# Second attention: the diagonal blocks of a chunk mirrored through VectorE and memory, and the turned tiles stored in pieces

## The chip, the cores and the metric

The kernel runs on one core of a Trainium2 chip. The metric is the device time of one execution in microseconds, where lower is better.

## What is computed

The input is x with 8 images of 128 channels and 48 x 48 pixels, that is 2304 tokens for each image. Two layers follow each other:

```python
# layer 0: causal attention over a group-normalised x, with leaky relu after each projection
q, k, v = (lrelu(W @ concat(gn(x), positions) + bias) for the three weights)
x = x + causal_softmax(q.T @ k / sqrt(128)) @ v
# layer 1: plain self attention, then a gated recurrence over the tokens
xh = layernorm(tokens(x))
t  = tokens(x) + softmax(xh @ xh.T) @ xh
wx = batchnorm(layernorm(t) @ W.T)
y[s] = sigmoid(wx[s] + y[s - 1] @ V.T)
out = t + y
```

What matters here is the second attention. Its scores are xh @ xh.T, with the same matrix on both sides, so they are symmetric, and so are their exponentials: the block of exponentials for key block m and query block n is the transpose of the block for key block n and query block m.

## The kernel before, in words

**Tiles.** An image has 2304 tokens in 18 blocks of 128 (P). Three blocks make a chunk of 384 (QC), so there are six chunks j = 0 to 5. Every matmul works on f32 tiles with 128 rows; a score tile is 128 keys by 384 queries, and the output of a chunk gathers in one PSUM tile `o` of 128 channels by 384 queries.

**Order of the work.** For each image the causal attention (class `Causal`) is followed by the second attention (class `Full`), chunk by chunk. The program makes one long list of items. For item n, `begin` issues a score matmul and an exponential on ScalarE (L1217 and L1219 in the second attention, L1018 and L1020 in the causal one). Three items later (LAG = 3) `product` issues the matmul that multiplies this tile into `o` (L1231, causal L1029). Everything else (projections, layer norms, residuals, stores) is put in chains of steps, with estimated costs and due times kept by class `Stream`; a step is emitted when its due time is reached, or earlier when something asks for its result (`st.finish`). The order on each engine is thus fixed when the program is built, and each engine runs its own list in order.

**Use of the symmetry before the change.** In chunk j the items of kind "direct" are those key blocks whose chunk n is at least j: their scores and exponentials are computed. The key blocks of earlier chunks are "turned" items. Their exponentials were computed already, as part of an earlier chunk, and only have to be transposed. The transpose goes in two halves. VectorE turns each 32 x 32 square of a direct tile (L1188) and puts the result in a tile `t`, which gathers three of them, 576 KB. The squares themselves change place by a trip through memory: `store` writes `t` to a DRAM tile `e` with one transfer (L1168), and `load` reads `e` back to a tile `g` with four transfers, one for each group of 32 partitions (L1159). The product of a turned item (L1227) reads `g` in place of a fresh exponential. There are 15 such pairs of chunks for each image. Two `t` tiles and three `g` tiles exist, so a transpose waits for the store of two tiles before, and a load waits for the products of three tiles before.

**The diagonal chunk.** The three key blocks of chunk j itself are direct items of full width: three score matmuls, three exponentials and three products of 384 columns each. The blocks behind the diagonal of this 3 x 3 square are computed twice, once on each side. For j > 0 these three items come last in their chunk.

**Transfers.** All transfers of the two attentions are issued by SyncE (SP), in order. Each transfer carries one of eight landing counters in turn, and in the built program it waits until the transfer that carried the same counter before it has landed. Between the attention and the recurrence each chunk also goes through `residual`, `rooted`, `spread` (three transfers `rs<-roots_t`, L1291, and four `t_d<-tt`, L1294), `fetch` (`t2x<-t_d`, L1298, and `scale<-rs`, L1300) and `product` (the matmul `wx<-t2x`, L1306, the ScalarE copy `t2c<-t2x`, L1327, and the VectorE product `scale<-wx`, L1307). The causal attention has a path of its own, `token_major`, that is of the same form as the new one: 192 KB to memory in one transfer (`o_d_c<-ot_c`, L966), then back in four of 48 KB (`to_c<-o_d_c`, L972). In `project`, VectorE adds the position term from PSUM to a work tile `z` (L884) and applies the leaky relu from `z` to its destination (L889).

Of the kernel before, what the change touches and what calls it, by code (L numbers as in the profile page):

```python
# [14 lines left out]
F32 = mybir.dt.float32  # L15
AF = mybir.ActivationFunctionType
ALU = mybir.AluOpType
# [587 lines left out]
def fast_path(ctx: ExitStack, tc: tile.TileContext, x, pe, w_ffn, out, x_tok, w_qkv, w_pos, v_t, gamma_beta, flag):  # L605
# [61 lines left out]
    with ExitStack() as actx:  # L667
# [24 lines left out]
        def chunk_tile(tag, name, holder=None, steps=0, bufs=2):  # L692

            if holder is not None:
                before = holders.setdefault(tag, deque([({}, 0)] * bufs))
                old, n = before.popleft()
                before.append((holder, steps))
                if "chain" in old:
                    st.advance(old["chain"], n)
            return (work if bufs == 2 else work1).tile([P, QC], F32, tag=tag, name=name)  # L700
# [154 lines left out]
        def project(b, n):  # L855

            cols = ts(n, QC)
            c = {}

            def normed():  # L860
                if n > 1:
                    st.finish(projected[b, n - 2])
                if (b, n) in pos_loads:
                    st.finish(pos_loads[b, n])
                c["pb"] = pos.pop((b, n))
                if n == 0:
                    keys[b] = big.tile([P, N], F32, tag="k", name=f"k_{b}")
                    vals[b] = big.tile([P, N], F32, tag="vT", name=f"vT_{b}")
                    largest[b] = small2.tile([P, 2, NQ], F32, tag="largest", name=f"largest_{b}")
                mg, rs = norm_of[b]  # L870
                c["xn"] = chunk_tile("xn", f"xn_{b}_{n}", c, 4)
                nc.vector.tensor_scalar(c["xn"], xbuf[b][:, cols], mg, rs, ALU.subtract, ALU.mult)  # L872

            def part(j):
                def f():
                    xn = c["xn"]
                    ps = psum_s(f"pj_{b}_{n}_{j}")
                    if j < 2:
                        nc.tensor.matmul(ps[:, :QC], wT[:, j, :], xn, start=True, stop=True)  # L879
                    else:  # L880
                        for m in range(0, QC, P):
                            nc.tensor.matmul(ps[:, ds(m, P)], xn[:, ds(m, P)], wT[:, j, :], start=True, stop=True)  # L882
                    z = chunk_tile("z", f"z_{b}_{n}_{j}")
                    nc.vector.tensor_add(z, ps[:, :QC], c["pb"][:, j, :])  # L884
                    if j == 0:
                        queries[b, n] = qp.tile([P, QC], F32, tag="q", name=f"q_{b}_{n}")
                    dst = (queries[b, n], keys[b][:, cols], vals[b][:, cols])[j]

                    nc.vector.scalar_tensor_tensor(dst, z, 0.01, z, ALU.mult, ALU.max)  # L889
                    c[j] = dst  # L890
                    if j == 2:
                        for i in range(2):
                            nc.vector.tensor_reduce(
                                largest[b][:, i, n : n + 1], c[i], AX.X, ALU.max, apply_absolute_value=True
                            )
                        load_positions(*divmod(b * NQ + n + 2, NQ))
                        if n + 1 < EARLY:
                            project(b, n + 1)
                        if n == NQ - 1 and b + 1 < B:
                            st.add([(partial(load_x, b + 1), 0.0, [])], 5.0)  # L900

                return f

            steps = [(normed, 0.0, [("DVE", 0.75)])]

            steps += [(part(j), QC * US, [("DVE", 0.0 if j < 2 else 4.5)]) for j in range(3)]
            c["chain"] = projected[b, n] = st.add(steps)
# [76 lines left out]
        def listed(chunks):  # L984
            return [(j, w, i == 0, i == len(ws) - 1) for j, ws in enumerate(chunks) for i, w in enumerate(ws)]
# [143 lines left out]
        class Full:  # L1129
# [12 lines left out]
            @staticmethod  # L1142
            def items():
                chunks = []
                for j in range(NQ):
                    behind = list(range(j + 1, NQ))
                    ahead = [("direct", QB * n + g) for n in ([0] + behind if j == 0 else behind + [j]) for g in range(QB)]
                    turn = [("turned", i, g) for i in range(j) for g in range(QB)]
                    both = [((k + 0.5) / len(ahead), w) for k, w in enumerate(ahead)]
                    both += [((k + 0.5) / len(turn), w) for k, w in enumerate(turn)]  # L1150
                    chunks.append([w for _, w in sorted(both, key=lambda e: e[0])])
                return listed(chunks)

            def load(self):
                i, j = self.pairs[len(self.loaded)]
                d, _ = self.stored[i, j]
                g = gpool.tile([P, R, QB, QB, SQ], F32, tag="g", name=f"g_{self.b}_{i}_{j}")
                for r in range(R):
                    nc.sync.dma_start(  # L1159
                        g[ts(r, SQ)].rearrange("c a j m r -> c a (j m r)"),  # L1160
                        d.rearrange("(a c) b f -> b c a f", a=R)[r],
                    )
                self.loaded[i, j] = g

            def store(self):
                j, n, t, at = self.to_store.popleft()
                d = dpool.tile([P, R, QB * QB * SQ], F32, tag=f"e_{j}_{n}", name=f"e_{self.b}_{j}_{n}")
                nc.sync.dma_start(d, t.rearrange("p b j m r -> p b (j m r)"))  # L1168
                self.stored[j, n] = d, max(at, st.now)

            def prefetch(self):
                while self.to_store and self.to_store[0][3] <= st.now:
                    self.store()
                n = len(self.loaded)
                if n < len(self.pairs) and n < self.used + 3 and self.pairs[n] in self.stored:
                    if self.stored[self.pairs[n]][1] + 6.0 <= st.now:
                        self.load()

            def turned(self, j, m, p, ready):

# [15 lines left out]
            def begin(self, j, what, first):  # L1196
                b = self.b
                if j == 0:
                    st.finish(normed_chunks[b, what[1] // QB])
                if first and b + 1 < B:  # L1200
                    if j == 1:
                        norm_chain[b + 1] = st.add(group_norm(b + 1))
                    if j == NQ - 2:
                        st.finish(norm_chain[b + 1])
                        project(b + 1, 0)
                self.prefetch()
                if what[0] == "turned":
                    i, g = what[1:]
                    while (i, j) not in self.loaded:
                        while self.pairs[len(self.loaded)] not in self.stored:  # L1210
                            self.store()
                        self.load()
                    return self.loaded[i, j][:, :, g, :, :].rearrange("p a m r -> p m a r"), 0.0
                m = what[1]
                xh = x_hat[b][1]
                s = psum_s(f"s1_{b}_{j}_{m}")
                nc.tensor.matmul(s[:, :QC], xh[:, ts(m, P)], xh[:, ts(j, QC)], start=True, stop=True)  # L1217
                p = pp.tile([P, QC], F32, tag="p", name=f"p1_{b}_{j}_{m}")
                nc.scalar.activation(p, s[:, :QC], AF.Exp, bias=shift)  # L1219
                return p, st.then(st.spend(QC * US), [("ACT", 0.5)])  # L1220

            def product(self, j, what, o, p, ready, first, last):
                xhT = x_hat[self.b][0]
                if what[0] == "turned":
                    i, g = what[1:]
                    out_ap = o[:, :QC].rearrange("p (m a r) -> p m a r", m=QB, a=R)
                    nc.tensor.matmul(out_ap, xhT[:, QB * i + g, :], p, start=first, stop=last)  # L1227
                    if g == QB - 1:
                        self.used += 1
                else:  # L1230
                    nc.tensor.matmul(o[:, :QC], xhT[:, what[1], :], p, start=first, stop=last)  # L1231
                    if what[1] // QB > j:
                        self.turned(j, what[1], p, ready)
                st.spend(QC * US, ready)

            def after(self, j, o):
                b = self.b
# [379 lines left out]
```

## Time and profile before

| | before |
|---|---|
| median of 3 runs | 1761.54 us (1758.81 to 1763.01) |
| the profiled execution's own time | 1763.07 us |
| span in its profile | 1761.4 us |
| TensorE matmul busy | 1733.7 us, 98% of the span |
| VectorE busy | 1159.5 us, 66% |
| ScalarE busy | 718.9 us, 41% |
| GpSimd busy | 321.0 us, 18% |
| mean granted TensorE clock | 0.991 |
| the 16 DMA engines: share of the queue that SyncE feeds | 50.3% |
| exponentials of the second attention (L1219) | 504, 580 ns each |
| exponentials of the causal attention (L1020), 384, 256 and 128 wide | 490, 384 and 277 ns each |
| transposes `t<-p` (L1188) | 360, 550 ns each |

The profile comes from one execution. "PE" is TensorE's matmul, "PEld" its weight load, "DVE" VectorE, "ACT" ScalarE, "POOL" GpSimd and "SP" SyncE; a "q" behind the name stands for the engine's queue of instructions that wait or issue transfers. A group of instructions is named by its source line, its engine and "what it writes <- what it reads". An f32 matmul of this kernel stands in the profile as two records, so a count of 1008 means 504 matmuls. Ends of matmuls are modelled and overlap the next, so the time that a matmul really takes is read from one start to the next.

### The profile page before, as it was taken

The numbers are of one execution on the slowest core, as the hardware profiler recorded it, in microseconds if no ns is written. First come the engines' busy times: TensorE is split into PE (matmuls) and PEld (weight loads), VectorE is DVE, ScalarE is ACT, GpSimd is POOL, SyncE is SP. The second block draws the span as 40 slices with busy tenths as digits, with TensorE's granted clock in tenths as the row PEclk, the third lists the DMA queues.
The fourth block names the chain that finished last, engine by engine and source line by source line (L and its number), as shares of the span: only waits on it lengthen the run. The fifth ranks groups of instructions, "written<-read, shape, count | busy, mean of one in ns | idle before, by whom it ended". The sixth has DMA issues, their size and how long they took to land.

```text
span 1761.4 us, 21442 instructions
## 1 busy us (share of the span) xinstructions
PE 1733.7 (98%) x6134; PEld 1082.0 (61%) x6135; DVE 1159.5 (66%) x3163; ACT 718.9 (41%) x1332; POOL 321.0 (18%) x397
## 2 busy tenths in 40 slices
PE   8999999999999999999999999999999999999986
PEld 5666666656666566666666566665666666665565
DVE  4875569655886459755696557864587556974357
ACT  2344334443344424443244433444344432444345
POOL 1131002300132001410024001320014100240006
PEclk7999999999999999999999999999999999999998
DMA  3415673157533684156731575335941568216768
GB/s 128 144 32 185 174 202 117 63 178 208 161 93 110 182 223 138 41 178 178 205 117 61 181 203 158 99 111 175 229 140 41 172 178 211 62 56 181 204 214 217
DMA packets 206050, 261.94 MB, mean 149 GB/s; under 512 B 90113, under 2 KB 175010, under 8 KB 205412
## 3 DMA queue, kind: packets, MB, share of 16 engines
q1 hardware_dynamic: 204972, 257.47, 50.3%
q0 software_dynamic: 720, 2.62, 1.0%
q8 instruction: 51, 0.84, 0.2%
q14 instruction: 75, 0.61, 0.1%
q10 hardware_dynamic: 232, 0.40, 0.1%
HBM read 150.24 MB, written 110.17 MB: 148 GB/s over the span
## 4 chain that ended last, share of the span: by engine, by line
PE 96%; DMA 1%; DVE 1%; SPq 1%; issue 0%; ACT 0%; POOL 0%; DVEq 0%; ACTq 0%; POOLq 0%
PE s L1217 18%; PE o L1231 18%; PE s L1018 17%; PE o L1029 17%; PE o L1227 13%; PE pj L879 4%; PE pj L882 2%; PE z L1530 2%; PE wx L1306 2%; PE tb L939 1%; PE of_t L939 1%; PE pb L837 0%; DMA x<-in_x_dram 0%; PE dn L1077 0%; DMA t2x<-t_d 0%; DMA out_dram<-r 0%
## 5 line engine op out<-in xcount | busy, mean ns | idle before, releaser
L1219 ACT ACTIVATE p<-s,shift 128x384 f32<-128x384 f32 x504 | 292.5, 580 | 519.0 <-PE s L1217 497.8
L1217 PE MATMUL s<-xh 128*128 128x384 f32 x1008 | 409.3, 488 | 0.0
L1020 ACT ACTIVATE p<-s 128x384 f32<-128x384 f32 (+2 forms) x504 | 231.0, 460 | 427.3 <-PE s L1018 349.3
L1231 PE MATMUL o<-p,xhT 128*128 128x384 f32 x1008 | 402.4, 486 | 1.1 <-ACT p L1219 1.1
L1018 PE MATMUL s<-q,k 128*128 128x384 f32 (+2 forms) x1008 | 382.9, 462 | 0.2 <-DVE k L889 0.2
L1029 PE MATMUL o<-p,vT 128*128 128x384 f32 (+2 forms) x1008 | 378.3, 457 | 0.0
L1227 PE MATMUL o<-g,xhT 128*128 128x384 f32 x720 | 281.4, 486 | 1.1 <-DMA g<-e 1.1
L1188 DVE STREAM_TRANSPOSE t<-p 128x384 f32<-128x384 f32 x360 | 186.1, 550 | 136.2 <-ACT p L1219 97.6
L1231 PEld LDWEIGHTS o<-p,xhT 128*128 128x128 f32 x1008 | 190.2, 190 | 129.2 <-ACT p L1219 1.7
L1217 PEld LDWEIGHTS s<-xh 128*128 128x128 f32 x1008 | 187.4, 190 | 119.5
L1029 PEld LDWEIGHTS o<-p,vT 128*128 128x128 f32 x1008 | 188.5, 191 | 116.1 <-POOL p L1023 3.0
L1018 PEld LDWEIGHTS s<-q,k 128*128 128x128 f32 x1008 | 182.3, 191 | 96.7 <-issue 1.3
L1044 DVE TENSOR_TENSOR acc<-acc,p 128x384 f32<-128x384 f32 (+2 forms) x408 | 213.4, 523 | 26.5 <-POOL p L1023 2.9
L1227 PEld LDWEIGHTS o<-g,xhT 128*128 128x128 f32 x720 | 134.1, 190 | 87.7 <-issue 1.8
L1023 POOL TENSOR_TENSOR p<-p,triu 128x128 f32<-128x128 f32 x144 | 77.8, 544 | 528.9 <-ACT p L1020 527.6
L884 DVE TENSOR_TENSOR z<-pj,pb 128x384 f32<-128x384 f32 x144 | 79.4, 551 | 137.5 <-PE pj L879 120.3
L1280 POOL TENSOR_TENSOR roots<-ve_f,mhalf 128x3 f32<-128x3 f32 x48 | 42.0, 876 | 500.7 <-DVE ve_f L923 500.7
L1114 POOL TENSOR_SCALAR xhT<-xhT 128x384 f32<-128x384 f32 x48 | 60.8, 1267 | 187.5 <-PE tb L939 187.5
L879 PE MATMUL pj<-xn,wT 128*128 128x384 f32 x192 | 80.6, 505 | 1.4 <-DVE xn L872 1.4
L1307 DVE TENSOR_TENSOR scale<-wx,scale 128x384 f32<-128x384 f32 x46 | 25.6, 556 | 69.2 <-PE wx L1306 59.9
L1258 DVE TENSOR_REDUCE dn<-of_t 128x3 f32<-128x384 f32 x48 | 26.6, 554 | 67.5 <-PE of_t L939 67.5
L1115 POOL TENSOR_SCALAR t1t<-t1t 128x384 f32<-128x384 f32 x48 | 61.3, 1277 | 0.0
(237 smaller groups left out, 1469.9 us busy)
## 6 DMA issues: line engine op xcount, KB each, us to landing
e<-t SPq DMA_DIRECT2D x120, 576.0 KB
g<-e SPq DMA_DIRECT2D x480, 144.0 KB
pb<-posb_d SPq DMA_DIRECT2D x46, 576.0 KB
t1t<-in_x_tok_dram SPq DMA_DIRECT2D x48, 192.0 KB
t_d<-tt SPq DMA_DIRECT2D x184, 48.0 KB
t2x<-t_d SPq DMA_DIRECT2D x46, 192.0 KB
scale<-rs SPq DMA_DIRECT2D x46, 192.0 KB
x<-in_x_dram SPq DMA_DIRECT2D x14, 576.0 KB
```

What stands on the lines that cost most here:

```text
L879: nc.tensor.matmul(ps[:, :QC], wT[:, j, :], xn, start=True, stop=True)
L884: nc.vector.tensor_add(z, ps[:, :QC], c["pb"][:, j, :])
L1018: nc.tensor.matmul(s[:, off:QC], keys[b][:, ts(m, P)], queries[b, j][:, off:], start=True, stop=True)
L1020: nc.scalar.activation(p[:, off:], s[:, off:QC], AF.Exp, scale=SCALE)
L1023: nc.gpsimd.tensor_mul(p[:, off : off + P], p[:, off : off + P], triu)
L1029: nc.tensor.matmul(o[:, off:QC], vals[b][:, ts(m, P)], p[:, off:], start=first, stop=last)
L1044: nc.vector.tensor_add(a[:, off:], a[:, off:], p[:, off:])
L1188: nc.vector.transpose(t[:, :, :, g, :].rearrange("p b j r -> p j b r"), p.rearrange("p (j b r) -> p j b r", j=QB, b=R))
L1217: nc.tensor.matmul(s[:, :QC], xh[:, ts(m, P)], xh[:, ts(j, QC)], start=True, stop=True)
L1219: nc.scalar.activation(p, s[:, :QC], AF.Exp, bias=shift)
L1227: nc.tensor.matmul(out_ap, xhT[:, QB * i + g, :], p, start=first, stop=last)
L1231: nc.tensor.matmul(o[:, :QC], xhT[:, what[1], :], p, start=first, stop=last)
```

## The change

(Lines of new steps are those of the changed kernel.) The diagonal chunk no longer computes both sides. Of its three key blocks, block g now covers only the query blocks g and after: the score matmul, the exponential and the direct product are 384, 256 and 128 columns wide (`offset`). What is missing are the blocks (0,1), (0,2) and (1,2), mirrored. For these, `mirror` lets VectorE turn the 32 x 32 squares of the first two tiles (L1187, one transpose of 128 x 256 and one of 128 x 128) into a tile `tm`; one transfer of 192 KB writes it to memory (`m<-tm`, L1200), and four of 48 KB read it back with the squares moved (`gm<-m`, L1203). These five transfers are issued by ScalarE. Two items of a new kind, "mirrored", stand at the end of each chunk; their products (L1271) are 128 and 256 columns wide and read `gm`.

The chunk's own three blocks now come first among its direct items. The turned tiles are now written in four transfers, one for each group of 32 partitions, each in rows of 1152 bytes (L1170), and read back in one, in rows of 4608 bytes (L1162). In `project` the tile `z` is gone: the sum is written to its destination, and the leaky relu works there in place.

```diff
-                    z = chunk_tile("z", f"z_{b}_{n}_{j}")
-                    nc.vector.tensor_add(z, ps[:, :QC], c["pb"][:, j, :])
...
-                    nc.vector.scalar_tensor_tensor(dst, z, 0.01, z, ALU.mult, ALU.max)
+                    nc.vector.tensor_add(dst, ps[:, :QC], c["pb"][:, j, :])
+                    nc.vector.scalar_tensor_tensor(dst, dst, 0.01, dst, ALU.mult, ALU.max)
...
-                    behind = list(range(j + 1, NQ))
-                    ahead = [("direct", QB * n + g) for n in ([0] + behind if j == 0 else behind + [j]) for g in range(QB)]
+                    ahead = [("direct", QB * n + g) for n in range(j, NQ) for g in range(QB)]
...
-                    chunks.append([w for _, w in sorted(both, key=lambda e: e[0])])
+                    order_of = [w for _, w in sorted(both, key=lambda e: e[0])]
+                    first = order_of.index(ahead[0])
+                    order_of.insert(0, order_of.pop(first))
+                    chunks.append(order_of + [("mirrored", g) for g in range(1, QB)])
...
+            @staticmethod
+            def offset(j, m):
+                return max(0, m - QB * j) * P if m < QB * (j + 1) else 0
 
             def load(self):
...
-                for r in range(R):
-                    nc.sync.dma_start(
-                        g[ts(r, SQ)].rearrange("c a j m r -> c a (j m r)"),
-                        d.rearrange("(a c) b f -> b c a f", a=R)[r],
-                    )
+                nc.sync.dma_start(g.rearrange("p a j m r -> p (a j m r)"), d.rearrange("p a f -> p (a f)"))
...
             def store(self):
...
-                nc.sync.dma_start(d, t.rearrange("p b j m r -> p b (j m r)"))
+                turned = d.rearrange("(b c) a f -> a c b f", b=R)
+                for r in range(R):
+                    nc.sync.dma_start(turned[r], t[ts(r, SQ)].rearrange("c b j m r -> c b (j m r)"))
...
+            def mirror(self, j, g, p, ready):
+
+                b, left = self.b, QB - 1 - g
+                if g == 0:
+                    self.tm = chunk_tile("tm", f"tm_{b}_{j}", bufs=1).rearrange("p (b q r) -> p b q r", b=R, q=QB)
+                first = g * (QB - 1)
+                nc.vector.transpose(
+                    self.tm[:, :, first : first + left, :].rearrange("p b q r -> p q b r"),
+                    p[:, (g + 1) * P :].rearrange("p (q b r) -> p q b r", q=left, b=R),
+                )
+                at = st.then(ready, [("DVE", 0.17 + left * 0.13)])
+                if g < QB - 2:
+                    return
...
+                def out_of():
+                    nc.scalar.dma_start(d, tm.rearrange("p b q r -> p b (q r)"))
+
+                def back_in(r):
+                    nc.scalar.dma_start(
+                        gm[ts(r, SQ)].rearrange("c a q r -> c a (q r)"), d.rearrange("(a c) b f -> b c a f", a=R)[r]
+                    )
+
+                steps = [(partial(back_in, r), 0.0, [("ACT", 0.4)]) for r in range(R - 1)]
+                steps = [(out_of, 0.0, [("ACT", 0.4), ("", 3.5)]), *steps, (partial(back_in, R - 1), 0.0, [("ACT", 0.4), ("", 3.5)])]
+                self.moved = st.add(steps, at + 0.6 - st.now)
...
+                if what[0] == "mirrored":
+                    st.finish(self.moved)
+                    return self.gm.rearrange("p a q r -> p q a r"), 0.0
                 m = what[1]
+                off = self.offset(j, m)
...
-                nc.tensor.matmul(s[:, :QC], xh[:, ts(m, P)], xh[:, ts(j, QC)], start=True, stop=True)
+                nc.tensor.matmul(s[:, off:QC], xh[:, ts(m, P)], xh[:, j * QC + off : (j + 1) * QC], start=True, stop=True)
...
-                nc.scalar.activation(p, s[:, :QC], AF.Exp, bias=shift)
+                nc.scalar.activation(p[:, off:], s[:, off:QC], AF.Exp, bias=shift)
...
+                elif what[0] == "mirrored":
+                    g = what[1]
+                    cols = g * P
+                    out_ap = o[:, :cols].rearrange("p (m a r) -> p m a r", m=g, a=R)
+                    nc.tensor.matmul(out_ap, xhT[:, QB * j + g, :], p[:, g - 1 : 2 * g - 1], start=first, stop=last)
                 else:
-                    nc.tensor.matmul(o[:, :QC], xhT[:, what[1], :], p, start=first, stop=last)
-                    if what[1] // QB > j:
+                    off = self.offset(j, what[1])
+                    cols = QC - off
+                    nc.tensor.matmul(o[:, off:QC], xhT[:, what[1], :], p[:, off:], start=first, stop=last)
+                    g = what[1] - QB * j
+                    if g >= QB:
                         self.turned(j, what[1], p, ready)
+                    elif g < QB - 1:
+                        self.mirror(j, g, p, ready)
```

More of the change, by code (lines that the diff above doesn't have):

```diff
@@ L1177, in prefetch @@
                         self.load()
+            def mirror(self, j, g, p, ready):
[10 more added lines that the diff above has]
+                    return
+                gm = chunk_tile("gm", f"gm_{b}_{j}", bufs=1).rearrange("p (a q r) -> p a q r", a=R, q=QB)
+                self.gm = gm
+                d = dpool.tile([P, R, QB * SQ], F32, tag=f"m_{j % 2}", name=f"m_{b}_{j}")
+                tm = self.tm
+                def out_of():
[7 more added lines that the diff above has]
+                self.moved = st.add(steps, at + 0.6 - st.now)
             def turned(self, j, m, p, ready):
@@ L1213, in begin @@
                     return self.loaded[i, j][:, :, g, :, :].rearrange("p a m r -> p m a r"), 0.0
+                if what[0] == "mirrored":
+                    st.finish(self.moved)
+                    return self.gm.rearrange("p a q r -> p q a r"), 0.0
                 m = what[1]
+                off = self.offset(j, m)
                 xh = x_hat[b][1]
                 s = psum_s(f"s1_{b}_{j}_{m}")
-                nc.tensor.matmul(s[:, :QC], xh[:, ts(m, P)], xh[:, ts(j, QC)], start=True, stop=True)
+                nc.tensor.matmul(s[:, off:QC], xh[:, ts(m, P)], xh[:, j * QC + off : (j + 1) * QC], start=True, stop=True)
                 p = pp.tile([P, QC], F32, tag="p", name=f"p1_{b}_{j}_{m}")
-                nc.scalar.activation(p, s[:, :QC], AF.Exp, bias=shift)
-                return p, st.then(st.spend(QC * US), [("ACT", 0.5)])
+                nc.scalar.activation(p[:, off:], s[:, off:QC], AF.Exp, bias=shift)
+                return p, st.then(st.spend((QC - off) * US), [("ACT", 0.17 + (QC - off) * 0.00085)])
             def product(self, j, what, o, p, ready, first, last):
@@ L1229, in product @@
                         self.used += 1
[L1230 to L1232 removed]
+                    cols = QC
+                elif what[0] == "mirrored":
[3 more added lines that the diff above has]
+                    nc.tensor.matmul(out_ap, xhT[:, QB * j + g, :], p[:, g - 1 : 2 * g - 1], start=first, stop=last)
+                else:
+                    off = self.offset(j, what[1])
[3 more added lines that the diff above has]
+                    if g >= QB:
                         self.turned(j, what[1], p, ready)
[L1234 removed]
+                    elif g < QB - 1:
+                        self.mirror(j, g, p, ready)
+                st.spend(cols * US, ready)
             def after(self, j, o):
```

## The prediction, made before the changed kernel ran

> **What bounds the kernel now.** I read the first part of the page, then the slices, the chain, the groups.
>
> ```profile
> PE 1733.7 (98%) x6134; PEld 1082.0 (61%) x6135; DVE 1159.5 (66%) x3163; ACT 718.9 (41%) x1332; POOL 321.0 (18%) x397
> ...
> PEclk7999999999999999999999999999999999999998
> ...
> PE 96%; DMA 1%; DVE 1%; SPq 1%; issue 0%; ACT 0%; POOL 0%; DVEq 0%; ACTq 0%; POOLq 0%
> ...
> L1231 PE MATMUL o<-p,xhT 128*128 128x384 f32 x1008 | 402.4, 486 | 1.1 <-ACT p L1219 1.1
> ...
> L1227 PE MATMUL o<-g,xhT 128*128 128x384 f32 x720 | 281.4, 486 | 1.1 <-DMA g<-e 1.1
> ```
>
> TensorE is the bound: 96% of the chain is its own, at nearly full clock, and its groups hardly ever sat idle (1.1 us each in the whole span). So a column of matmul saved is time saved, unless a new wait appears. What a column costs stands in the order of time (TensorE, causal attention):
>
> ```profile
> 57.16 0.59 PE L1029 MATMUL o<-p,vT 128*128 128x256 f32 x2
> 57.59 0.81 PE L1018 MATMUL s<-q,k 128*128 128x384 f32 x2
> 58.24 0.38 PE L1029 MATMUL o<-p,vT 128*128 128x128 f32 x2
> 58.46 0.81 PE L1018 MATMUL s<-q,k 128*128 128x384 f32 x2
> ```
>
> From start to start: 0.43 us for 256 columns, 0.65 for 384 (0.645 over longer runs), 0.22 for 128. It is proportional; narrow matmuls carry no extra.
>
> Next the queue that feeds the turned tiles: SyncE from chunk 3 to chunk 4 of the fourth image, then memory by chunk (stretches of chunks 3 and 4; last columns clock, DMA share, GB/s).
>
> ```profile
> 821.21 3.01 SPq L1337 DMA_DIRECT2D t2l_d<-t2c  x1
> 824.31 1.57 SPq L1291 DMA_DIRECT2D rs<-roots_t  x3
> 825.93 1.86 SPq L1294 DMA_DIRECT2D t_d<-tt  x4
> 827.89 0.38 SPq L1168 DMA_DIRECT2D e<-t  x1
> 828.36 4.22 SPq L1159 DMA_DIRECT2D g<-e  x8
> ```
>
> ```profile
> 808.20:827.30 19.10, 19.10 (x63) 11.35 (x62) 8.03 (x24) 7.97 (x13) 0.85 (x1) 1.00 0.63 159
> 827.30:848.30 21.00, 21.00 (x77) 13.05 (x76) 13.48 (x34) 6.12 (x9) 0.85 (x1) 1.00 0.96 230
> ```
>
> SyncE issues without a gap for over 11 us, and memory is 96% busy in chunk 4. Setting each load's landing (the last update of its counter in the trace) against its first product, the median margin over 8 images is 1.3 us for pair (1,4), 1.9 for (2,4), 1.1 for (2,5), and 8 or more in chunks 0 to 3. TensorE is covered, but thinly, in chunks 4 and 5. The `wx<-t2x` matmul has margins of 5 to 10 us in chunks 0 to 3 of an image.
>
> **What the Trainium skill says.** "TensorE: Matmul & The Clock Gate", Back-to-back issue gap: in a stream of weight loads and matmuls a narrow one costs more than its share. The trace disagrees (0.22 against 0.65 us), so the trace is used. "DMA: Bandwidth & Descriptors", Anatomy of one DMA: a wait for a semaphore happens on the issuing sequencer before dispatch. The trace agrees: the waits list has SyncE waiting 32.3 us in 18 waits for `o_d_c<-ot_c`. On ScalarE such a wait will hold the exponentials behind it. The same page, Issuing engines are not separate DMA queues: all issuers share the same 16 engines, so a second issuer saves only issue time. No run here shows it.
>
> **Part by part.**
>
> *Matmul columns.* A diagonal chunk had 3 scores and 3 products of 384, that is 2304. It now has 768 of scores, 768 of direct and 384 of mirrored products, 1920. 384 fewer, 48 chunks: 48 x 0.645 = 31.0 us off TensorE. Six matmuls become eight, which by the proportion above costs nothing.
>
> *ScalarE.* Two of three exponentials shrink. By L1020's widths (490, 384, 277 ns) that is 0.32 us a chunk, 15 us in all, hidden. Added are 240 issues, 0.36 us for the 192 KB form (ScalarE's own `wT` load) and 0.43 for the 48 KB form (`to_c`, median): 2.1 us a chunk, 100 in all. At 41% busy there is room. Behind them wait exponentials, whose products are due three items later: 1.9 us in turned stretches, 3.9 in direct ones, less 0.8 for hand-over and exponential. Singly the issues fit; four in a row (1.7 us) come only where the next exponential belongs to the next chunk. I take nothing; if a landing is awaited for over 2 us there, the excess is TensorE's.
>
> *VectorE.* `t<-p` at 384 takes 550 ns, a 32-wide one (L1285) 183; in proportion 0.42 and 0.28. 48 x 0.70 = 34 us, 66% becomes 68%. Hidden; the DVE was idle over a third of these stretches. If late, `m<-tm` waits and ScalarE with it. Dropping `z`: same two operations, nothing, and a few nanoseconds either way at most.
>
> *The mirror's latency.* The `o_d_c`/`to_c` pair has the same sizes: landing 1.6 us after the end of the issue (90% under 2.6), then 1.57 after the last of four (90% under 2.9). In the built order chunks 0 and 1 have a margin. In chunk 3 the last exponential is given off about 3.0 us before the mirrored product; four issues take 1.7, landing 1.6: 0.3, say 0.4 us late. Chunks 2 and 4 come out even, chunk 5 a little early, except at the end of the last image, where nothing follows: 1.5 us late. Low end zero; with the 90% value 1.3 us more in each of four chunks, 5 us an image.
>
> *Stores and loads.* A store goes from one issue (0.38) to four (1.8), a load from four to one. Sum equal: 0. In chunks 4 and 5 there are about 9 loads and 3 stores, so SyncE gains some 8 us of issue there. Packets of 1152 bytes hold an engine 78 ns, of 4608 bytes 206 (mean of the trace's packet records), so a load costs 512 x 78 / 16 = 2.5 us before and 128 x 206 / 16 = 1.65 after; chunk 4's 96% falls to about 75%. Stores get 0.85 dearer in chunks 0 to 2, with DMA shares of 0.36 to 0.60. `t` is freed 2 us later: VectorE already waits 37.3 us for `e<-t`; six `p` buffers cover 3 items more. Nothing on the path.
>
> *What is late next.* The built order shows two new ties. A transfer waits for the one eight before it, and ScalarE's now count among them, so SyncE, which ran 6 to 14 us ahead of TensorE, must wait for transfers that ScalarE issues at TensorE's pace. And the chunk's own blocks come first, so stores stand directly ahead of loads. Pair (1,4): its product moves from 94.6 us after the image's first score to 89.8 (2.6 from four shorter chunks, 2.2 from order). Ahead of its load: the third `rs` waits for the mirror's first read of chunk 3, done at 83.5; four `t_d` 1.9, four stores 1.8, issue 0.35, landing 3.4 to 4.1 (`pb<-posb_d`, same 576 KB form: quiet 3.4, median 4.1). Sum 91.0 to 91.7, late by 0.8 to 1.5 after chunk 3's 0.4; I take 1.1. Pair (2,5): four stores behind late transposes, `t2x`, `scale`, then 3.8: 0 to 1, take 0.4. `t2x` of chunk 0, used in chunk 2: behind two fourfold stores, the second bound to `m<-tm`: 0 to 1, take 0.4.
>
> *Sum.* Give-back for an image 0.4 + 1.1 + 0.4 + 0.4 = 2.3 us, times 8 is 18.4, and 1.5 at the end: 19.9. 1763.1 (span 1761.4 and 1.7 around it) - 31.0 + 19.9 = 1752.0. This run stood 1.5 above the median of the runs shown, so 1750.5, rounded to 1750.
>
> **The rivals.** *Nearly all is kept.* For it: lighter memory in chunk 4 may bring landings to the quiet end, and TensorE's own delays let SyncE catch up. At 0.3 us an image plus 1.5: 1763.1 - 31.0 + 3.9 - 1.5 = 1734.5.
>
> *Slower: the lock-step of two queues.* ScalarE waits for SyncE's landings and SyncE for ScalarE's, through the shared counters; each late landing moves the loads of chunks 3 to 5. For it: SyncE's gapless run, margins of 1.1 to 1.9, five links a chunk. Against it: in the trace the transfer eight back had landed over 5 us before ScalarE's place in 95% of places. It decides from 31.0 / 8 = 3.9 us an image. With each of the waits above 1 us longer (landings near their 90% values) and chunks 2 and 4 late as well, 5.5 us an image: 1763.1 - 31.0 + 44 - 1.5 = 1774.6.
>
> *No change*: 3.5 to 4.3 us an image, 1758 to 1765. That the change doesn't do what it says can't be: the built order has 384 columns fewer in each chunk.
>
> **Numbers.** 0.2% is about what a measurement of this kernel can tell from no change (3.5 us). Partly kept, 1740 to 1758: 0.36. Nearly all kept: 0.20. Same: 0.10. Slower: 0.34, because several places with thin margins must all hold. So faster 0.56, and the time is 1750. The range goes from 1733 to 1774, leaving out a sliver of the best case and nearly half of the slower one; the likeliest case's own range is 1740 to 1758.
>
> **What would show it.** Right: TensorE's busy time without idle falls by 31; L1271 waits for `gm<-m` under 1 us a chunk; L1263 waits for `g<-e` about 12 us in all, in chunk 4; DMA share of chunk 4 near 0.75. Wrong: exponentials (L1255) waited for by products for more than a few us; the `wx` matmul waiting for `t2x` over 1 us an image; waits for `g<-e` in chunks 1 to 3.

## The result and the profile after

The changed kernel takes 1810.94 us in the median of 4 runs (1806.44 to 1816.5). The kernel before takes 1760.17 us on the same chip (1758.35 to 1763.01). The ratio is 1.0289 with a 95% interval of 1.0264 to 1.0315, so the change costs 51 us, where a gain of 11 was forecast (1761.54 to 1750). The profiled execution took 1816.5 us, with a span of 1814.8 us.

The first part, the chain and the groups that matter, from the page of the changed kernel (last columns of a group: busy time and mean of one, then idle time before it and what ended it):

```profile
PE 1725.2 (95%) x6327; PEld 1098.6 (61%) x6327; DVE 1185.4 (65%) x3259; ACT 699.3 (39%) x1332; POOL 319.2 (18%) x397
...
PE 76%; DMA 16%; SPq 3%; DVE 2%; issue 1%; ACT 0%; ACTq 0%; POOL 0%; DVEq 0%; POOLq 0%
...
L1275 PE MATMUL o<-p,xhT 128*128 128x384 f32 (+2 forms) x1008 | 371.6, 457 | 3.4 <-ACT p L1255 3.4
L1263 PE MATMUL o<-g,xhT 128*128 128x384 f32 x720 | 286.8, 497 | 36.9 <-DMA g<-e 36.9
L1220 DVE STREAM_TRANSPOSE t<-p 128x384 f32<-128x384 f32 x360 | 184.1, 550 | 165.4 <-DMA e<-t 141.0
```

TensorE's own share of the chain fell from 96% to 76%, and 16% are now transfers. The product of the turned tiles (L1263) stood still 36.9 us where it had waited 1.1 us before. The other two lines are there for what they don't show: late exponentials cost the direct product 3.4 us, once, and waits of VectorE for stores, 141 us here, turn out below to cost nothing of themselves.

Where the turned tiles come late is seen in SyncE's queue, in the same place of the fourth image as in the prediction (the changed kernel in order of time; start, length):

```profile
836.15 0.34 SPq L1162 DMA_DIRECT2D g<-e  x1
842.39 0.40 SPq L1383 DMA_DIRECT2D out_dram<-t2c  x1
842.84 2.14 SPq L1384 DMA_DIRECT2D t2l_d<-t2c  x1
845.08 1.57 SPq L1338 DMA_DIRECT2D rs<-roots_t  x3
846.69 1.86 SPq L1341 DMA_DIRECT2D t_d<-tt  x4
848.65 1.82 SPq L1170 DMA_DIRECT2D e<-t  x4
850.57 0.38 SPq L1162 DMA_DIRECT2D g<-e  x1
```

From 836.49 to 842.39 SyncE issues nothing. What it waits for is in the waits list of its queue (total, times, longest):

```profile
SPq L1170 <- DMA gm<-m: 39.7, 36, 6.3
SPq L1383 <- DMA m<-tm: 39.6, 7, 5.8
SPq L1170 <- DMA m<-tm: 38.8, 7, 6.6
SPq L1338 <- DMA gm<-m: 25.4, 14, 3.7
```

The store of `out` (L1383) needs nothing that the mirror made. It carries the landing counter that `m<-tm` carried before it, and so it waits until that write of ScalarE's has landed, in seven images of eight for about 5.7 us. (Here `m<-tm`, issued at 836.17, landed at 842.33, and the store went out at 842.39.) Behind it stand 8 us of issues, and then the load of pair (1,4). On TensorE that is the stall at 855.69 (start, length, idle before):

```profile
852.34 0.38 PE L1253 MATMUL s<-xh 128*128 128x128 f32 x2
852.56 0.60 PE L1275 MATMUL o<-p,xhT 128*128 128x256 f32 x2
855.69 1.69 PE L1263 MATMUL o<-g,xhT 128*128 128x384 f32 x4 [2.54 <-DMA g<-e]
857.17 1.49 PE L882 MATMUL pj<-wT,xn 128*128 128x128 f32 x6
858.45 1.49 PE L1253 MATMUL s<-xh 128*128 128x384 f32 x2
859.73 0.63 PE L1275 MATMUL o<-p,xhT 128*128 128x128 f32 x2
860.16 0.93 PE L1353 MATMUL wx<-t2x,w1T 128*128 128x384 f32 x2
```

Two things are to be seen. The wait is 2.54 us. And after it the score matmul of 384 columns at 858.45 takes 1.28 us to the next start, not 0.645: TensorE runs at half speed for a while (the last section has the clock).

### The profile page after: what moved, and what is told of

Read it like the earlier page. It is cut to its first block, busy times and chain, and to the rows that moved or that the text cites. A ratio compares the mean times of both kernels' runs of the same rounds, so it can differ in the third digit from the quotient of the medians.

```text
span 1814.8 us, 22185 instructions
## 1 busy us (share of the span) xinstructions
PE 1725.2 (95%) x6327; PEld 1098.6 (61%) x6327; DVE 1185.4 (65%) x3259; ACT 699.3 (39%) x1332; POOL 319.2 (18%) x397
## 4 chain that ended last, share of the span: by engine, by line
PE 76%; DMA 16%; SPq 3%; DVE 2%; issue 1%; ACT 0%; ACTq 0%; POOL 0%; DVEq 0%; POOLq 0%
PE s L1016 16%; PE o L1027 16%; PE s L1253 13%; PE o L1275 12%; DMA g<-e 7%; PE o L1263 7%; DMA gm<-m 3%; PE pj L879 3%; DMA m<-tm 2%; DMA t2x<-t_d 2%; PE pj L882 2%; PE z L1577 2%; PE o L1271 2%; PE wx L1353 1%; SPq L1170 1%
## 5 line engine op out<-in xcount | busy, mean ns | idle before, releaser
L1255 ACT ACTIVATE p<-s,shift 128x384 f32<-128x384 f32 (+2 forms) x504 | 274.3, 550 | 588.3 <-PE s L1253 469.4
L1253 PE MATMUL s<-xh 128*128 128x384 f32 (+2 forms) x1008 | 381.7, 461 | 0.0
L1275 PE MATMUL o<-p,xhT 128*128 128x384 f32 (+2 forms) x1008 | 371.6, 457 | 3.4 <-ACT p L1255 3.4
L1263 PE MATMUL o<-g,xhT 128*128 128x384 f32 x720 | 286.8, 497 | 36.9 <-DMA g<-e 36.9
L1263 PEld LDWEIGHTS o<-g,xhT 128*128 128x128 f32 x720 | 133.9, 193 | 120.4 <-DMA g<-e 47.1
L886 DVE TENSOR_TENSOR q<-pj,pb 128x384 f32<-128x384 f32 x48 | 26.7, 556 | 94.1 <-PE pj L879 89.1
L927 POOL TENSOR_TENSOR rs_c<-ve_c,mhalf 128x3 f32<-128x3 f32 x48 | 48.4, 1008 | 75.3 <-DVE ve_c L921 75.3
L1271 PE MATMUL o<-gm,xhT 128*128 128x128 f32 x192 | 46.0, 336 | 13.5 <-DMA gm<-m 11.0
```

What stands on the lines that cost most here:

```text
L1253: nc.tensor.matmul(s[:, off:QC], xh[:, ts(m, P)], xh[:, j * QC + off : (j + 1) * QC], start=True, stop=True)
L1255: nc.scalar.activation(p[:, off:], s[:, off:QC], AF.Exp, bias=shift)
L1271: nc.tensor.matmul(out_ap, xhT[:, QB * j + g, :], p[:, g - 1 : 2 * g - 1], start=first, stop=last)
L1275: nc.tensor.matmul(o[:, off:QC], xhT[:, what[1], :], p[:, off:], start=first, stop=last)
```

## The experiments

Four theories were held against each other. A: the two queues are tied through the shared counters, so SyncE falls to the pace of ScalarE's transfers. B: the new form of store and load does it. C: the order with the chunk's own blocks first does it. D: the trip of the mirrored squares is simply too long. M (bytes), S (ScalarE held up) and O (the planner's new order for SyncE) joined later. All times are medians of 4 runs, `swap_alone` of 20 and `mirror_on_tensor` of 12; the ratio is to the kernel before, which stood at 1759.9 to 1760.9 us beside them.

| kernel | us | ratio, 95% interval |
|---|---|---|
| swap_alone | 1757.3 | 0.9979 to 0.9993 |
| order_alone | 1771.6 | 1.0043 to 1.0076 |
| mirror_alone | 1856.6 | 1.0533 to 1.0568 |
| no_trip | 1729.6 | 0.9805 to 0.9838 |
| mirror_on_gpsimd | 1791.2 | 1.0154 to 1.0188 |
| mirror_on_sync | 1832.0 | 1.0385 to 1.0420 |
| trip_unused | 1810.2 | 1.0249 to 1.0309 |
| trip_in_two | 1780.3 | 1.0093 to 1.0127 |
| plan_only | 1743.6 | 0.9871 to 0.9916 |
| trip_small | 1796.6 | 1.0161 to 1.0229 |
| count_only | 1805.1 | 1.0231 to 1.0266 |
| mirror_on_tensor | 1764.4 | 1.0016 to 1.0040 |
| trip_kept_order | 1823.3 | 1.0341 to 1.0382 |
| gpsimd_kept_order | 1795.6 | 1.0147 to 1.0207 |
| tensor_kept_order | 1744.5 | 0.9884 to 0.9917 |

### The parts one by one

`swap_alone`, on the kernel before (the same in `load`, reversed):

```diff
-                nc.sync.dma_start(d, t.rearrange("p b j m r -> p b (j m r)"))
+                turned = d.rearrange("(b c) a f -> a c b f", b=R)
+                for r in range(R):
+                    nc.sync.dma_start(turned[r], t[ts(r, SQ)].rearrange("c b j m r -> c b (j m r)"))
```

> The kernel before, with only the form of the turned tiles' transfers changed: store in four transfers, load in one. No mirror, full-width diagonal, old order. Theory A (the new transfers of ScalarE tie SyncE to TensorE's pace, so loads of turned tiles come late): the swap needs the tie to hurt, so 1757 to 1765 us, waits for g<-e under 5 us. Theory B (the swap itself: four stores stand ahead of the loads, and t is freed later): 1780 to 1800 us, with L1220's counterpart waiting over 100 us for e<-t. Theory C (own blocks first): as A, 1757 to 1765.

1757.3 us: theory B is out for the swap by itself. The waits that looked costly are there all the same (page of `swap_alone`):

```profile
L1186 DVE STREAM_TRANSPOSE t<-p 128x384 f32<-128x384 f32 x360 | 183.4, 548 | 166.6 <-DMA e<-t 114.9
L1225 PE MATMUL o<-g,xhT 128*128 128x384 f32 x720 | 281.3, 487 | 0.9 <-DMA g<-e 0.9
```

VectorE waits 114.9 us for stores (37.3 before) and TensorE notices nothing. VectorE is not the bottleneck.

`order_alone`, on the kernel before:

```diff
-                    behind = list(range(j + 1, NQ))
-                    ahead = [("direct", QB * n + g) for n in ([0] + behind if j == 0 else behind + [j]) for g in range(QB)]
+                    ahead = [("direct", QB * n + g) for n in range(j, NQ) for g in range(QB)]
```

> The kernel before, with only the order changed: the chunk's own three key blocks come first among its direct items, full width, no mirror, transfers as before. Theory A: 1758 to 1766 us. Theory B: 1757 to 1765. Theory C (own blocks first put the finished t tiles, and so their stores, directly ahead of the loads for chunks 4 and 5): 1775 to 1800 us, with waits for g<-e of over 15 us.

1771.6 us, between A's and C's figures: with loads in four pieces the order alone costs 12 us. Together with the new loads it costs next to nothing, as `no_trip` shows.

`mirror_alone` is the changed kernel with the old `store` and `load`, the two edits of `swap_alone` turned round.

> The changed kernel with the old form of the turned tiles' transfers: store in one transfer, load in four. Mirror, narrow matmuls and own-first order stay, ScalarE issues the mirror's transfers. Theory A: the tie is whole, 1795 to 1815 us. Theory B: the loss goes, 1735 to 1755 us. Theory C: 1790 to 1810.

1856.6 us, worse than A expected. B is refuted in sign as well: under the tie the new form of the transfers saves 46 us (1856.6 - 1810.9). Its lines in the waits list of SyncE's queue:

```profile
SPq L1163 <- DMA g<-e: 50.1, 66, 2.7
...
SPq L1163 <- DMA gm<-m: 36.3, 11, 5.4
```

A load in four pieces carries four counters, so it waits for others four times. That the saving comes from there alone was not separated.

`no_trip`, on the changed kernel (the DRAM tile, the five transfers and their steps go too; cut here):

```diff
-                gm = chunk_tile("gm", f"gm_{b}_{j}", bufs=1).rearrange("p (a q r) -> p a q r", a=R, q=QB)
-                self.gm = gm
...
-                self.moved = st.add(steps, at + 0.6 - st.now)
+                self.gm = self.tm
```

> The changed kernel without the mirror's five transfers: the mirrored products read VectorE's tile of turned squares directly, so their squares are in the wrong places, which leaves that part of the computation out. Everything else stays (narrow matmuls, own-first order, store in four, load in one). Theory A: with the tie gone nearly the whole saving shows, 1730 to 1742 us. Theory B: the loss of the swap stays, 1785 to 1805 us. Theory C: likewise 1780 to 1800.

1729.6 us, as A had it. The page of `no_trip`:

```profile
PE 1703.0 (99%) x6327; PEld 1099.2 (64%) x6327; DVE 1186.1 (69%) x3259; ACT 698.5 (40%) x1332; POOL 309.6 (18%) x397
...
PE 97%; DVE 1%; DMA 1%; ACT 0%; issue 0%; POOL 0%; SPq 0%; ACTq 0%; POOLq 0%; DVEq 0%
...
L1247 PE MATMUL o<-g,xhT 128*128 128x384 f32 x720 | 278.3, 487 | 0.8 <-DMA g<-e 0.8
```

TensorE is busy 30.7 us less than before (1733.7), and the time fell by 30.3 (from 1759.9 beside it). The whole saving is there, with the narrow matmuls, the own-first order, VectorE's transposes and the new stores and loads all in. What takes it away is the trip, with the steps that plan it. In the profiled executions `no_trip` and the changed kernel are 86 us apart. TensorE's stalls are 68 us longer in the changed kernel, by the starts of its matmuls, and slow matmuls after stalls cost it 12.5 us more (last section). That accounts for 81 of the 86.

### What of the trip it is

`mirror_on_sync` and `mirror_on_gpsimd` change who issues the five transfers (`nc.sync` or `nc.gpsimd` for `nc.scalar`).

> The changed kernel with the mirror's five transfers issued by SyncE. Theory A: SyncE now waits for tm and for m in its own order, so it is tied to TensorE's pace in the same way, 1790 to 1840 us. Theory D: 1795 to 1820. Theory M: 1800 to 1815. Theory S: ScalarE is free of it, 1730 to 1745 us.

> The changed kernel with the mirror's five transfers issued by GpSimd, whose transfers carry eight landing counters of their own in the built program. Theory A (tie of SyncE to ScalarE through the shared counters): the tie is gone while bytes and trip stay, 1730 to 1745 us. Theory D (the trip's own latency: the mirrored product waits for gm): 1795 to 1820 us, as GpSimd is no faster. Theory M (the 18.9 MB of new traffic slow the other transfers): 1800 to 1815. Theory S (ScalarE held up by issues and waits, so exponentials are late): 1730 to 1745.

On SyncE 1832.0 us: with ScalarE free of the transfers it is no better. As late exponentials cost only 3.4 us in the changed kernel too, S is out, and the tie is the same or worse. Here the stall sits at the mirrored product, 71.4 us of waiting for `gm<-m` at L1271, and only 2.1 us for `g<-e`. On GpSimd 1791.2 us, 19.7 better than on ScalarE but 46 above the top of what A allowed. The trace shows one cause at once: in each of seven images the mirrored product of chunk 5 comes 4.2 to 4.6 us late, together 30.8 us, because GpSimd's list has the mask of the next image's first causal tile ahead of that chunk's transfers. The rest shows when this run is set beside `plan_only` (further down), for SyncE's list is the same in both, and also the changed kernel's. With other counters the stalls before pair (1,4) and before `t2x`, 24.8 and 11.7 us in the changed kernel, are gone (0 and 0.2). Beyond `plan_only` there are the late `gm`, 4 us more of stalls before the pairs (2,4) and (2,5), and 9.5 us more of slow matmuls after stalls, together 44 us, which is the difference of the two profiled executions. That leaves at most those 4 us to the bytes of the trip.

`trip_unused`, on the changed kernel:

```diff
-                    return self.gm.rearrange("p a q r -> p q a r"), 0.0
+                    return self.tm.rearrange("p b q r -> p q b r"), 0.0
```

> The changed kernel with all five transfers as they are, but the mirrored products read VectorE's tile of turned squares and not the tile that came back, so the squares are in the wrong places and nothing on TensorE waits for the trip. Theory A: the tie stays, 1785 to 1811 us, with waits for g<-e of over 50 us. Theory D: 1728 to 1740 us. Theory M and theory S: 1795 to 1811.

1810.2 us: D is out. Taking away the waits for `gm<-m`, 17 us in the changed kernel, gains 0.7 us, inside the spread. TensorE waits longer for `g<-e` instead (45.0 us at L1263, 36.9 in the changed kernel; A had asked for over 50) and for `t2x` (12.4 at L1353 for 9.5), and slow matmuls after stalls cost it 7 us more. A wait removed ahead of a queue that is late anyway comes back at the next places.

`trip_in_two` reads `m` back in one transfer; `trip_small` keeps all five, but of 12 KB each, and does not use them (the write is shown, the reads likewise):

```diff
-                    nc.scalar.dma_start(d, tm.rearrange("p b q r -> p b (q r)"))
+                    nc.scalar.dma_start(d[0:SQ, 0, :], tm[0:SQ, 0].rearrange("p q r -> p (q r)"))
```

> The changed kernel with the mirror's way back in one transfer of 192 KB, which leaves the squares in the wrong places: two transfers a chunk on ScalarE in place of five, same bytes. Theory A: two ties a chunk in place of five, 1750 to 1785 us. Theory D: the product still waits for a trip of the same length, 1795 to 1815. Theory M: same bytes, 1800 to 1815. Theory S: 1760 to 1785.

> The changed kernel with all five transfers of a chunk on ScalarE, with the same waits for one another and the same counters, but of 12 KB each in place of 192 and 48 KB, and the mirrored products reading VectorE's tile, so that part of the computation is left out. SyncE's list is the changed kernel's. Theory A: the number of transfers and their waits do it, 1795 to 1811 us. Theory M (bytes): what plan_only gives and up to 10 us more, under 1775.

With two transfers 1780.3 us, with five small ones 1796.6. This points to the number of transfers and not to their bytes: a sixteenth and a quarter of the bytes save 14 us, three transfers less save 31. (SyncE's list in `trip_in_two` is another one, so this pair is no clean slope, and 1780.3 lies in S's range as well as in A's.)

`plan_only` keeps the steps in the plan and lets them issue nothing (`pass` for the two calls); `count_only` issues five transfers of 4 KB from a constant tile, that wait for no data:

```diff
-                    nc.scalar.dma_start(d, tm.rearrange("p b q r -> p b (q r)"))
+                    nc.scalar.dma_start(d[0:SQ, 0, 0:SQ], ident[0:SQ, 0:SQ])
```

> The changed kernel with the mirror's steps kept in the plan (same costs and due times) but issuing no transfer, and the mirrored products reading VectorE's tile of turned squares, so the way through memory is left out of the computation. SyncE's list of transfers is then the same, entry by entry, as in the changed kernel, which it isn't in the kernel without the steps (there the two stores of out and t2l, 3.4 us of issue, stand behind the load of pair (1,4), here ahead of it). Theory A (tie of the queues): 1728 to 1740 us. Theory O (the order that the planner gives SyncE makes the loads late): 1755 to 1785 us, with pair (1,4) and (2,5) late.

> The changed kernel with five transfers of 4 KB a chunk in the places of the old ones on ScalarE, from a constant tile: they carry counters and wait for counters, but for no data. The mirrored products read VectorE's tile, so that part of the computation is left out. Theory A in its strict form (the counters alone tie the queues): 1785 to 1811 us. Theory A in its wider form (the counters tie SyncE to transfers that land late because they wait for turned squares and for each other): 1740 to 1770. Theory O: as plan_only.

This pair settles it, since SyncE's list is entry by entry the changed kernel's in both traces. `plan_only`: 1743.6 us, so the other order alone costs 14 us, 3.6 more than A allowed and 11 less than O asked. `count_only`: 1805.1 us. Five transfers of 4 KB a chunk, which depend on no data of the computation, cost 61.5 us, as the strict form of A said. No product waits for an exponential over 0.15 us in that trace, so it isn't ScalarE's issues that hold TensorE up. Waits list of SyncE's queue in `count_only`:

```profile
SPq L1170 <- DMA m<-ident: 69.8, 42, 5.3
...
SPq L1162 <- DMA m<-ident: 49.8, 7, 7.4
...
SPq L1336 <- DMA m<-ident: 27.2, 15, 3.4
```

Stores, loads and `rs` wait for transfers that they have nothing to do with. From one start of TensorE to the next, less the width's own time, the stalls before a first product come to (sums over 8 images, us):

| before the first product of | no_trip | plan_only | count_only | changed kernel |
|---|---|---|---|---|
| pair (1,4) | 0 | 0.5 | 22.9 | 24.8 |
| pair (2,4) | 1.0 | 5.7 | 3.7 | 7.5 |
| pair (2,5) | 0 | 9.2 | 16.0 | 7.8 |
| `t2x` | 0.4 | 0.8 | 23.3 | 11.7 |
| `gm` | - | - | - | 17.0 |

### Ways out

`mirror_on_tensor` lets TensorE turn the three blocks:

```diff
-                nc.vector.transpose(
...
+                tp = psum_t(f"mt_{b}_{j}_{g}")
+                for q in range(left):
+                    nc.tensor.transpose(tp[:, ts(q, P)], p[:, ts(g + 1 + q, P)], ident)
+                st.spend(left * P * US / 2)
+                nc.vector.tensor_copy(self.gm[:, first * P : (first + left) * P], tp[:, : left * P])
```

> The changed kernel with the three blocks of a chunk turned by TensorE (three transposes of 128 columns) and copied out of PSUM by VectorE; no transfer, no trip, narrow matmuls, own-first order and the new form of store and load stay. Theory A: no tie, so the saving without the trip, 1729.6 us, plus 48 x 3 x 0.11 = 15.8 us of transposes on TensorE: 1743 to 1750 us. Theory O: the order of SyncE's list is another one again and has out and t2l ahead of the load of pair (1,4): 1755 to 1775.

1764.4 us, 14 above A's range and inside O's. Its transposes take 15.7 us from start to start (48 times 0.218 for two and 0.109 for one), as worked out, so the rest had to be elsewhere. The kernels with the old order kept tell where:

> TensorE's way to mirror, with its transposes not counted in the plan, so that SyncE's list is that of the kernel without the trip. If the order made the 15 us too much: 1729.6 + 15.7 of transposes = 1745, 1743 to 1749 us. If the transposes themselves or the copies cost more than their time from start to start: 1758 to 1766.

> The changed kernel with the mirror's five transfers on ScalarE, whole and used, but issued at fixed items (the write one product after the second turned block, the four reads five to eight products after it) and not through the planner, so that SyncE's list of transfers is entry by entry that of the kernel without the trip. Theory A (the tie through counters is nearly all): 1785 to 1811 us. Theory O (the order has a large part in it when the queues are tied): 1740 to 1770 us.

> The same with the five transfers issued by GpSimd: whole trip, whole computation, counters of its own, SyncE's list that of the kernel without the trip, and chunk 5's transfers ahead of the next image's masks on GpSimd. Theories A and O together: the saving of the kernel without the trip less a few us for bytes and late gm, 1731 to 1745 us. If bytes or GpSimd's own issue were what cost 26 us before: 1755 to 1790.

`tensor_kept_order` (the `st.spend` dropped, so that SyncE's list is that of `no_trip`) takes 1744.5 us, 14.9 above `no_trip`: the transposes and nothing else. It computes everything, and it beats both kernels: the one before by 1.0% (0.8 to 1.2), the changed one by 66 us. So the order that the planner made for `mirror_on_tensor`, a third one, costs 20 us. `trip_kept_order` takes 1823.3 us, above A's range: with the good order the tie is no cheaper, so of the changed kernel's loss O is only the 14 us that `plan_only` shows. `gpsimd_kept_order`, at 1795.6 us, missed its figure by 50 us, so the counters are not the only tie. GpSimd and SyncE of this kernel in order of time:

```profile
834.81 0.56 POOL L1204 DMA_DIRECT2D gm<-m  x1 [3.29 <-DMA m<-tm]
835.38 0.87 POOL L1335 TENSOR_TENSOR roots<-ve_f,mhalf 128x3 f32<-128x3 f32 x1
```

```profile
829.82 0.32 SPq L1163 DMA_DIRECT2D g<-e  x1
836.53 1.56 SPq L1346 DMA_DIRECT2D rs<-roots_t  x3
```

GpSimd waits 3.29 us for `m<-tm` to land, and `roots` stands behind that wait. `roots_t` needs `roots`, SyncE's `rs` needs `roots_t`, and the loads stand behind `rs`: SyncE stands still from 830.14 to 836.53. It is the same lock-step over another engine, and pair (2,4) is late by 33 us in all. Late `gm` (13 us) and slow matmuls after stalls (22 us) make up most of the rest of the 72 us between this trace and that of `no_trip`.

## Why the prediction was wrong, step by step

- *Columns, 31.0 us.* Right: 30.3 in `no_trip`.
- *ScalarE, VectorE, nothing.* Right for both: `no_trip` has VectorE's part, and the direct product's wait for exponentials in the changed kernel is 3.4 us.
- *Stores and loads, nothing on the path.* Right: `swap_alone` is 0.1% faster. The DMA share of chunk 4 came out at 0.86 in `no_trip`, not 0.75, without harm.
- *The mirror's latency.* Mis-sized. The landing of `m<-tm` was taken as 1.6 us, from the causal stretch. By the counters' updates it is 1.54 us in chunks 0, 1 and 5, but 5.69 in chunk 3 and 3.18 in chunk 4 (medians, from the end of the issue). At 836.17 ScalarE issues it 0.02 us after a load of 576 KB and behind a store of 576 KB. The Trainium skill ("DMA: Bandwidth & Descriptors", Issuing engines are not separate DMA queues) says that all issuers share the same 16 engines; the prediction quoted it, and then priced the transfer as if it had them for itself. The 5.69 us agree with the page, though no run here takes the transfers around it away. In `gm` stalls that is 2.1 us an image for the 0.4 forecast, though `trip_unused` shows that this wait by itself is not what costs.
- *What is late next.* This is the step that failed: it put 1.9 of its 2.3 us an image here, as three single late landings, and did not carry the tie of the counters through SyncE's whole list. Its sum for pair (1,4) started from the third `rs`, bound to ScalarE's first read at 83.5 us after the image's first score, and added 1.9, 1.8 and 0.35 us of issues. The moment was right: SyncE was let go at 842.39, which is 83.1 us after that score. But it was stopped earlier in its list, at the store of `out`, so `out`, `t2l` and `rs`, 4.3 us of issue that the sum had as done, were still to come. 83.1 + 4.3 + 1.9 + 1.8 + 0.4 is 91.5 (in the median the issue ended at 92.0), the landing took 4.7 and not 3.4 to 4.1, and the load was there at 96.5 (median) and not at 91.0 to 91.7. TensorE, late itself, came to this product at 93.9 and not at 90.2. The stall is 3.1 us an image for the 1.1 forecast; the `t2x` stalls are 1.5 for 0.4, pair (2,5) 1.0 for 0.4, and pair (2,4), 0.9, was not seen. With `gm` that is 8.6 us an image where 2.3 were put. TensorE's half speed after stalls, 12.5 us in all or 1.6 an image, comes on top; the prediction had no term for it.
- *The slower rival*, given 0.34, was this mechanism, at 5.5 us an image; the runs show about 10 (1810.9 - 1729.6, for 8 images). What spoke against it was misread: the places where the transfer eight back had long landed were counted where ScalarE waits for SyncE. The harm runs the other way, and before the change nothing in the trace could show it, for in the two attentions SyncE shared its counters with nobody.
- *The planner.* The prediction read the built order but did not price that order against another. `plan_only` puts 14 us on it.

The sum by runs: 1760.2 - 30.6 (to `no_trip`) + 14.1 (order) + 61.5 (five counters) + 5.8 (data, bytes, `gm`) = 1811. The last two terms can shift against each other by some 10 us, since `trip_small`, with data waits, is faster than `count_only`, without.

Of the signs called wrong, one came true: the `wx` matmul waited for `t2x` over 1 us an image (L1353, 9.5 us of idle time in all). Waits for `g<-e` in chunks 1 to 3 did not appear, and exponentials were late once, for 3.4 us.

## What to carry to other kernels

Before giving transfers to a second engine, look at what counts their landings: a queue that runs ahead loses its lead when it shares counters with a queue that keeps the pace of the compute, however small the transfers are (4 KB in `count_only`). Follow each wait in both directions, and list what stands in order behind the waiting instruction, on SyncE as on GpSimd. And where a planner orders the queue, run once with the steps planned but empty: it tells the price of the new order from that of the work.

## What was unexpected of the hardware

A stall can cost more than its length. The stretches of the changed kernel around the stall above (busy times, then granted clock, DMA share, GB/s):

```profile
855.60:857.10 1.50, 1.41 (x4) 0.87 (x5) 0.00 (x0) 0.00 (x0) 0.00 (x0) 0.96 1.15 379
857.10:858.40 1.30, 1.30 (x7) 1.23 (x6) 0.00 (x0) 0.00 (x0) 0.00 (x0) 0.50 0.95 220
858.40:859.70 1.30, 1.30 (x4) 0.73 (x3) 0.97 (x2) 0.00 (x0) 0.00 (x0) 0.50 0.99 312
859.70:860.90 1.20, 1.20 (x5) 0.93 (x4) 1.07 (x3) 0.92 (x2) 0.00 (x0) 0.71 0.84 342
```

The granted clock falls to 0.50 at 856.99, 1.3 us after the stall has ended, and stays there for 3.41 us. The Trainium skill ("TensorE: Matmul & The Clock Gate", Part 1: The HAM clock gate) has the clock halved after an idle window of about 3.4 us and free again after a busy one. The length agrees, but here 2.54 us without a matmul were enough, while the longer stall that ended at 643.42 (2.97 us) was not followed by a lower clock.

The traces show what tells them apart. In every trace of this case the clock changes only on a grid of steps of 3.41 us. The first stall put 2.12 us of idle time into one step; the second lay across a border and put 1.50 and 1.47 us into two. I took TensorE's idle time step by step in all 17 traces, from 60 us after the start to 80 us before the end. Each of the 95 steps at full clock after which it fell to 0.50 held at least 1.92 us without a matmul, and none after which it stayed held more than 2.01. It came back after the first step with less than 0.6 us idle. (The ends of matmuls are modelled, so these borders are rough.)

In the changed kernel 63 matmul records fall in such slow steps, from 60 us after the start to 75 us before the end, and take 12.5 us more than at full rate; before the change, and in `no_trip`, there are none in that stretch. The mean clock was 0.984 where it had been 0.991.
